# Reordering the steps of a pipelined graph network: one-hots and GpSimd operations placed anew

## The chip, the cores and the metric

The kernel runs on one core of one Trainium2 chip. The metric is the device time in microseconds, the median over several runs. One core has five engines with instruction queues of their own: PE (TensorE), DVE (VectorE), ACT (ScalarE), POOL (GpSimd) and SP (SyncE, here used for DMA only). Instructions of one engine run in the order in which the program issues them; between engines they are ordered by semaphores.

## The reference

128 graphs with 128 nodes and 64 features each. `x` is (128, 128, 64) and `adj` (128, 128, 128), symmetric in its pattern, with about 6% of the edges present and all self-loops. H is 192.

```python
mask = (adj > 0.0)
xj_proj = x @ W1a                                   # W1a, W1b: the halves of W1
diff = x[:, :, None, :] - x[:, None, :, :]
h  = relu(xj_proj[:, :, None, :] + diff @ W1b + b1)
hm = einsum('bjkh,bjk->bjh', h, mask)
x  = layernorm(x + hm @ W2 + sum(mask, -1)[..., None] * b2)    # layer 0

agg = adj @ x
out = elu(elu(agg @ V1 + c1) @ V2 + c2) @ V3 + c3              # 64 -> 128 -> 128 -> 64
x   = layernorm(x + out)                                       # layer 1
```

## The kernel before

**Tiling.** Two graphs make a pair; there are 64 pairs (`NP`). In layer 0 only the edges that exist are computed. For each pair the nodes are sorted by degree. The sorted nodes fall into nine blocks (`BLOCKS`), each with a fixed number of neighbour slots. For each block a one-hot matrix (`oh`, L707, written by VectorE in bf16 from `vp`, the running number of each neighbour, and `slotc`, the slot numbers) selects the neighbours.

**A unit** is one block of one pair: ScalarE writes the nodes' own part `aj` into a PSUM bank, repeated over the slots (L955), TensorE adds the neighbours' part by matmuls with the one-hots (L966, the parts `cf`, `rest` and `low` of a number split into three bf16 terms), and VectorE sums absolute values over the slots (L976). relu(z) is (z + |z|)/2, so a correction (`sa`, `ea`, `corr`) turns the sum of absolute values into the sum of relus. Three PSUM banks serve the units in turn, so a unit's write by ScalarE waits for the reduce of the unit three before.

**Threads.** What a pair needs is written as threads of steps:

- `prepare`: `mk` and the degrees (L576, VectorE), `degb` and `keyc` (L583, L584, GpSimd), a matmul that spreads the keys, the comparisons `cmp` (L597, VectorE), and the permutation `perm` (L605, VectorE).
- `sort_x`: sorted x, the projections to `aj` (L643, ScalarE), `sa` (L651, GpSimd), a short matmul, `ea` (L668, VectorE), `corr` (L674, GpSimd).
- `sort_mask`: the sorted mask, its prefix sums `vp` (L700, ScalarE), and the nine one-hots.
- `turn` and `project_c`: transposes, the neighbours' projections, `cf` (L756, ScalarE), `rest` (L760, VectorE), `low` (L764, GpSimd).
- `finish`: `hm` (L889), the product with W2, the way back to the old order of nodes, the normalization (`norm`: y L772 and st L777 on VectorE, `ve` L784, `rs` L787 on GpSimd, the scaling `x`), then layer 1 (`aggregate`, L917, two rounds of `elu` with `r`, `e`, `up` on ScalarE and `h` L841 on GpSimd), the last matmuls and the second normalization to `o`, which SyncE stores.

Work of about eight pairs is in flight at a time. For pairs from `LATE` on, `hm`, `ve`, `x` and `h` run on VectorE instead of GpSimd (`h` at L844, `x` at L801), and `o` is shared by ScalarE (L818) and VectorE (L804).

**The order.** A planner (`Flow`) runs while the program is built. It repeatedly takes the thread whose next step is due first, gives it an estimated time on its engine and emits its instructions. The due time of a step is `ROUND * p` plus an entry of the table `DUE`; `finish` of the last six pairs adds the offsets of `LAST`. The engine name "PORT" is a pseudo-engine of the planner's estimates: steps that name it are kept apart in its plan, but not on the chip. The plan sets nothing but the order of the instructions in each queue and which of the five `m` banks in PSUM a step takes.

```python
self.clock[e] = t + cost
...
due = [due[i] + later[0 if i < 4 else 1 if i < 8 else 2 if i < 16 else 3]
       for i in take]
flow.start(ROUND * p, due, gen)
```

Of the kernel before, what the change touches and what calls it, by code (L numbers as in the profile page):

```python
# [47 lines left out]
def gnn_kernel(ctx: ExitStack, tc: tile.TileContext, x, adj, w1, b1, w2, b2,  # L48
# [28 lines left out]
    with ExitStack() as fast:  # L77
        loads = fast.enter_context(tc.tile_pool(name="loads", bufs=8))
        prep = fast.enter_context(tc.tile_pool(name="prep", bufs=5))
        work = fast.enter_context(tc.tile_pool(name="work", bufs=5))  # L80
        ps_e = fast.enter_context(tc.tile_pool(name="ps_e", bufs=1, space=bass.MemoryType.PSUM))
        ps_m = fast.enter_context(tc.tile_pool(name="ps_m", bufs=1, space=bass.MemoryType.PSUM))
        K = sparse(tc, locals())
# [103 lines left out]
def sparse(tc, env):  # L187

    g = type("env", (), dict(env))
    nc, P, N, F, H, O, HB, H1, NP, E = (  # L190
        g.nc, g.P, g.N, g.F, g.H, g.O, g.HB, g.H1, g.NP, g.E)
# [11 lines left out]
    AHEAD = 4  # L203

    DUE = {
        "prepare": (-21.4113, -21.4103, -20.8009, -20.0167, -16.5154),
        "sort_x": (-11.5423, -11.5413, -2.7266, -2.3845, 0.0214, 1.3277, 2.8168, 12.6347),
        "sort_mask": (-10.347, -9.218, -8.7754, -8.3524, -5.8935, -5.758, -5.757, -5.756,
            -5.755, -5.754, -5.1217, -5.1207, 1.0998, 1.1008),
        "turn": (-26.2816, -24.1632),  # L210
        "project_c": (-13.6709, -12.5698, -12.2977, -12.2751, -11.3882, -10.0036, -8.4866),
        "finish": (13.0404, 22.189, 23.0263, 23.6287, 24.5439, 27.278, 28.4137, 32.117, 34.5413,
            35.4475, 35.4637, 36.1308, 36.1318, 36.1328, 37.7091, 43.35, 43.6764, 45.3519,
            45.5256, 46.0637, 48.8402, 49.096, 49.261, 51.6959, 51.9284),
        "unit": [(-1.48, -0.1838, 0.7496), (0.1062, 0.9216, 0.9226), (0.3987, 1.0968, 1.978),
            (1.1956, 1.4908, 2.221), (2.1682, 2.6234, 3.9141), (2.1874, 3.6496, 4.2699),
            (2.4467, 4.3465, 5.2271), (8.5772, 9.7062, 10.187), (5.7368, 9.4611, 10.7836)],
        "consts_late": (14.79, 24.13, 25.63, 26.63, 26.78, 26.79, 26.8, 26.81, 26.82, 27.82,
            28.82, 29.82, 30.82, 31.82, 32.82, 33.82, 34.82, 35.82, 36.82, 37.82, 38.82, 39.82,
            40.82),  # L220
    }

    LATE = NP - 2
    LAST = ((-3.5, -9.4, -4.9, -1.3), (5.5, -4.3, 0.3, 7.6), (-0.9, -2.8, 3.8, 7.6), (0.1, -0.2, -0.4, 5.1), (0.0, -1.6, 0.0, 0.2), (0.0, 0.0, 0.2, 0.0))

    def begin_thread(name, p, gen):
        due = DUE[name]
        if name == "finish":
            take = range(25)
            if p >= LATE:  # L230
                take = (0, 1, 2, 3, 4, 5, 6, 6, 7, 8, 9, 10, 11, 12, 14, 15, 16, 17, 19,
                        20, 21, 22, 22, 23, 24, 24)
            k = NP - 1 - p
            later = LAST[k] if k < len(LAST) else (0.0,) * 4
            due = [due[i] + later[0 if i < 4 else 1 if i < 8 else 2 if i < 16 else 3]
# [104 lines left out]
    def made(*names):  # L340
        return [event("const", name) for name in names]
# [425 lines left out]
    def norm(p, yps, ev, name, rest, shift):  # L767
# [31 lines left out]
        def apply(v, s):  # L799
# [3 lines left out]
            else:  # L803
                v.tensor_scalar(o[:, s, :], y[:, s, :], rs[:, s:s + 1], None, op0=OP.mult)  # L804
        if p < LATE:
            ev, = yield ("POOL", 1.1, [ev] + made("mhalf"), 0,
# [17 lines left out]
    def elu(p, zb, ev, name, k):  # L824
# [10 lines left out]
        h = work.tile([P, 2 * N], F32, name=name)  # L835
        if p < LATE:
            up = work.tile([P, 2 * N], F32, name="up", bufs=3)
# [11 lines left out]
    def overflow():  # L849


        v, B = nc.vector, 2 * NP

        over = slotc[:, :NB * B].rearrange("p (n b) -> p n b", n=NB)

        def before():
            for i, (p0, p1, sl) in enumerate(BLOCKS):
                v.memset(first[:, i:i + 1], float(p0))
        ev, = yield ("DVE", 0.5, [[0.0]], 0, before)

        def compare(blocks):
            for i in blocks:
                v.tensor_scalar(over[:, i, :], g.degs, float(BLOCKS[i][2]), None, op0=OP.is_gt)
        for k in range(0, NB, 3):
            ev, = yield ("DVE PORT", 0.5, [ev], 0, lambda: compare(range(k, k + 3)))

        def rows_over(t):
            for i in range(NB):
                nc.tensor.matmul(t[:B, i:i + 1], over[:, i, :], onesb[:, 0:1], start=True, stop=True)
        ev, t = yield ("PE", 0.6, [ev], 1, rows_over)  # L870
        ev, = yield ("DVE", 0.1, [ev], 0, lambda: v.tensor_tensor(hit[:B], t[:B, :NB], first[:B],
                                                                  op=OP.is_gt))
        flow.give(t, ev)
        ev, = yield ("DVE", 0.1, [ev], 0, lambda: v.tensor_reduce(bad[:B], hit[:B], AX.X, OP.max))
        ev, t = yield ("PE", 0.1, [ev], 1, lambda t: nc.tensor.matmul(
            t[:1, :B], bad[:B], identb[:B, :B], start=True, stop=True))
        ev, = yield ("DVE", 0.2, [ev], 0, lambda: v.tensor_reduce(
            count, t[:1, :B].rearrange("o (n s) -> o n s", s=2), AX.X, OP.max))
        ev, = yield ("DVE", 0.2, [ev], 0, lambda: v.tensor_reduce(some, t[:1, :B], AX.X, OP.max))
        flow.give(t, ev)  # L880

    def finish(p):

        d, xx = S[p], XX[p]
        hm = work.tile([P, 3, N], F32, name="hm", bufs=4)
        late = p >= LATE
        ev, = yield ("DVE PORT" if late else "POOL PORT", 0.47 if late else 1.05,
# [16 lines left out]
        if p == NP - 1:  # L904
            due = [DUE["finish"][i] + LAST[0][2] + 0.5 for i in (8, 12, 14, 16)]
            flow.start(ROUND * p, due[:1] * 4 + due[1:2] * 3 + due[2:3] + due[3:] * 2, overflow())
# [327 lines left out]
```

## Time and profile before

| what | us |
|---|---|
| median of 3 runs | 699.7 (699.24 to 699.98) |
| the profiled execution's own time | 699.37 |
| its span in the trace | 697.6 |
| first gather of pair 0 | 18.09 |
| first gather of pair 7 | 92.34 |
| first gather of pair 62 | 655.85 |
| first gather of pair 63 | 665.64 |
| end of the last unit's reduce | 676.92 |
| end of the span | 697.6 |

The span runs from the first to the last event that the profiler saw. A round is the time from a pair's first gather to that of the next pair. In a profile's row, a name such as `e<-oh,cf` says what is written and from what; the number in `x6` is the number of instructions. Mean granted clock of TensorE is 0.992.

The two engines with the most work follow each other closely: PE is busy for 97% of the span and DVE for 97%, ACT for 89% and POOL for 84%.

### The profile page before, as it was taken

Reading aid. Unit: us, or ns where it says so; the run is one execution under the profiler, and the core shown is the slowest. Engines: PE = TensorE matmul, PEld = TensorE weight load, DVE = VectorE, ACT = ScalarE, POOL = GpSimd, SP = SyncE. Lnnn points to the kernel's source line nnn. Section 1 sums busy time; section 2 is a strip of 40 time slices with the busy share of each in tenths; the row PEclk is TensorE's granted clock in tenths of the full one; section 3 lists DMA queues with packets and bytes.
Section 4 is the critical chain, followed back from the end, with each engine's and each line's share of the span. In section 5 each row is a group of like instructions: output and inputs, shape, how many; then the busy total and the mean of one; then the engine's idle time right before and its main releaser. Section 6 shows DMA issues by size and latency. Waiting matters only on the chain.

```text
span 697.6 us, 40860 instructions
## 1 busy us (share of the span) xinstructions
PE 676.6 (97%) x17245; PEld 610.3 (87%) x17246; DVE 674.2 (97%) x2267; ACT 621.2 (89%) x1731; POOL 583.4 (84%) x983
## 2 busy tenths in 40 slices
PE   7989999999999999999999999999999999999984
PEld 4878999999999999999999999999999999989972
DVE  6899999999999999999999999999999999999985
ACT  3678999999999999999999999999999999999963
POOL 5447988988988898898899889899888888899873
PEclk9999999999999999999999999999999999999996
DMA  3200111110110111111011011101101101100000
GB/s 93 56 3 3 35 26 27 35 34 19 34 34 19 33 34 26 27 34 34 19 35 33 23 31 34 32 20 34 34 19 33 34 23 30 35 22 9 12 9 20
DMA packets 54988, 20.01 MB, mean 29 GB/s; under 512 B 37904, under 2 KB 54800, under 8 KB 54800
## 3 DMA queue, kind: packets, MB, share of 16 engines
q1 hardware_dynamic: 54096, 17.06, 10.1%
q8 instruction: 137, 2.24, 1.3%
q14 instruction: 51, 0.42, 0.2%
q10 hardware_dynamic: 704, 0.30, 0.2%
HBM read 13.14 MB, written 4.19 MB: 25 GB/s over the span
## 4 chain that ended last, share of the span: by engine, by line
PE 90%; DVE 4%; POOL 2%; ACT 2%; issue 1%; DMA 1%; SPq 0%; POOLq 0%; DVEq 0%; ACTq 0%
PE e L966 46%; PE m L263 23%; PE m L741 4%; PE m L636 3%; PE m L722 3%; PE m L917 2%; PE m L619 2%; PE m L632 2%; DVE sums L976 1%; PE m L657 1%; PE m L661 1%; PE m L723 1%; POOL rs L787 1%; ACT e L955 1%; DVE oh L707 1%
## 5 line engine op out<-in xcount | busy, mean ns | idle before, releaser
L955 ACT COPY e<-aj 128x504 f32<-128x504 f32 (+6 forms) x576 | 311.3, 551 | 39.1 <-DVE sums L976 36.9
L976 DVE TENSOR_REDUCE sums<-e 128x54 f32<-128x486 f32 (+8 forms) x576 | 336.8, 603 | 3.5 <-PE e L966 2.1
L966 PE MATMUL e<-oh,cf 128*64 128x162 bf16 (+6 forms) x3456 | 210.9, 229 | 4.3 <-ACT e L955 4.0
L966 PE MATMUL e<-oh,rest 128*64 128x162 bf16 (+6 forms) x3456 | 209.0, 227 | 0.0
L966 PE MATMUL e<-oh,low 128*64 128x162 bf16 (+6 forms) x3456 | 209.0, 227 | 0.0
L966 PEld LDWEIGHTS <-cf 128*64 128x64 bf16 x3456 | 150.3, 110 | 30.7 <-issue 29.8
L707 DVE TENSOR_TENSOR oh<-vp,slotc 128x336 bf16<-128x336 bf16 (+6 forms) x576 | 155.9, 325 | 0.3 <-ACT vp L700 0.3
L966 PEld LDWEIGHTS <-rest 128*64 128x64 bf16 x3456 | 141.4, 110 | 0.0
L966 PEld LDWEIGHTS <-low 128*64 128x64 bf16 x3456 | 141.1, 110 | 0.3 <-POOL low L764 0.3
L841 POOL TENSOR_TENSOR h<-up,e 128x256 f32<-128x256 f32 x124 | 95.9, 774 | 10.4 <-ACT up L839 10.3
L787 POOL TENSOR_TENSOR rs<-ve,mhalf 128x2 f32<-128x2 f32 x128 | 92.0, 719 | 13.9 <-DVE ve L784 3.5
L764 POOL TENSOR_TENSOR low<-rest 128x512 bf16<-128x512 f32 x64 | 66.6, 1040 | 9.8 <-DVE rest L760 9.8
L651 POOL TENSOR_TENSOR sa<-aj,srow 128x384 f32<-128x384 f32 x64 | 65.6, 1025 | 8.1 <-DVE perm L605 4.0
L889 POOL TENSOR_TENSOR hm<-sums,corr 128x384 f32<-128x384 f32 x62 | 62.3, 1005 | 4.9
L674 POOL TENSOR_TENSOR corr<-ea,sa 128x384 f32<-128x384 f32 x64 | 65.3, 1020 | 0.0
L831 ACT ACTIVATE r<-m,cc 128x256 f32<-128x256 f32 x128 | 61.8, 483 | 3.5 <-PE m L263 3.3
L839 ACT ACTIVATE up<-m,cc 128x256 f32<-128x256 f32 x124 | 58.0, 468 | 0.0
L834 ACT ACTIVATE e<-r 128x256 f32<-128x256 f32 x128 | 53.4, 417 | 2.2
L760 DVE TENSOR_TENSOR rest<-m,cf 128x256 f32<-128x256 f32 x128 | 51.9, 407 | 0.0
L784 POOL TENSOR_SCALAR ve<-st 128x2 f32<-128x2 f32 x124 | 33.6, 271 | 20.5 <-DVE st L777 9.6
L756 ACT COPY cf<-m 128x256 f32<-128x256 f32 x128 | 41.4, 377 | 7.2 <-PE m L263 5.5
L643 ACT ACTIVATE aj<-m,b1n 128x128 f32<-128x128 f32 x128 | 40.0, 364 | 3.7 <-PE m L636 2.2
(163 smaller groups left out, 1459.4 us busy)
## 6 DMA issues: line engine op xcount, KB each, us to landing
adj<-in_adj_dram SPq DMA_DIRECT2D x64, 128.0 KB, 2.5
xx<-in_x_dram SPq DMA_DIRECT2D x64, 64.0 KB, 2.2
out_dram<-o SPq DMA_DIRECT2D x64, 64.0 KB, 1.7
w1s<-in_L_gnn_W_dram ACTq DMA_DIRECT2D x2, 96.0 KB, 2.9
w2s<-in_L_gnn_W_dram ACTq DMA_DIRECT2D x2, 48.0 KB, 2.5
v2s<-in_L_gnn_W_dram SPq DMA_DIRECT2D x1, 64.0 KB, 2.1
v1d<-in_L_gnn_W_dram SPq DMA_DIRECT2D x2, 32.0 KB, 2.0
rows<-in_L_gnn_b_dram SPq DMA_DIRECT2D x1, 64.0 KB, 5.5
```

The lines of the kernel that those rows point to most:

```text
L263: nc.tensor.matmul(out[h], lhsT[:, h], rhs, **kw)
L651: evs, = yield ("POOL PORT", 1.0, [have] + made("srow"), 0, lambda: nc.gpsimd.tensor_mul(sa, aj, srow))
L674: ev, = yield ("POOL PORT", 1.05, [ev, evs], 0, lambda: nc.gpsimd.tensor_sub(corr, ea, sa))
L707: lambda: nc.vector.tensor_tensor(oh[:, 2 * base:2 * (base + n)].rearrange("p (b s w) -> p b s w", b=2, w=w), vp[:, :, p0:p1].rearrange("p ...
L764: lambda: nc.gpsimd.tensor_sub(flat(low), flat(rest), upper(flat(rest))))
L787: nc.gpsimd.tensor_tensor(rs, ve, mhalf, op=OP.pow)
L831: lambda: nc.scalar.activation(r, z, AF.Relu, bias=c, scale=-1.0))
L841: ev, = yield ("POOL PORT", 0.64, [ev, evr], 0, lambda: nc.gpsimd.tensor_add(h, up, e))
L889: lambda: (nc.vector if late else nc.gpsimd).tensor_sub(hm, d["sums"], d["corr"]))
L955: lambda: nc.scalar.copy(e.rearrange("p (c s w) -> p c s w", c=3, w=w), d["aj"][:, :, p0:p1].rearrange("p c (o w) -> p c o w", o=1) .to_br ...
L966: nc.tensor.matmul(e[HALVES[h], c * n:(c + 1) * n], cp(k, s, slice(chunk * HB, (chunk + 1) * HB)), oh[:, 2 * base + s * n:2 * base + (s + ...
L976: nc.vector.tensor_reduce(d["sums"][:, :, p0:p1], e.rearrange("p (c s w) -> p c w s", c=3, w=w), AX.X, OP.add, apply_absolute_value=True)
```

## The change

The tables of due times are replaced, `LATE` becomes `NP - 3`, and the offsets `LAST` are new. No other line changes.

```diff
     DUE = {
-        "prepare": (-21.4113, -21.4103, -20.8009, -20.0167, -16.5154),
-        "sort_x": (-11.5423, -11.5413, -2.7266, -2.3845, 0.0214, 1.3277, 2.8168, 12.6347),
-        "sort_mask": (-10.347, -9.218, -8.7754, -8.3524, -5.8935, -5.758, -5.757, -5.756,
-            -5.755, -5.754, -5.1217, -5.1207, 1.0998, 1.1008),
-        "turn": (-26.2816, -24.1632),
-        "project_c": (-13.6709, -12.5698, -12.2977, -12.2751, -11.3882, -10.0036, -8.4866),
...
+        "prepare": (-28.364, -26.9206, -21.7812, -19.6952, -16.1672),
+        "sort_x": (-10.9988, -6.9662, -5.6912, -4.4256, -4.4082, -2.3787, -2.259, 9.8274),
+        "sort_mask": (-10.5624, -9.3935, -7.0848, -6.4931, -5.7683, -4.7121, -4.6732, -4.6722,
+            -4.6712, -4.6702, -4.6692, -4.6472, -4.5393, 5.8821),
+        "turn": (-28.2283, -26.8089),
+        "project_c": (-16.5622, -15.4251, -15.3192, -15.3182, -14.9622, -14.9612, -12.1988),
...
-    LATE = NP - 2
-    LAST = ((-3.5, -9.4, -4.9, -1.3), (5.5, -4.3, 0.3, 7.6), (-0.9, -2.8, 3.8, 7.6), (0.1, -0.2, -0.4, 5.1), (0.0, -1.6, 0.0, 0.2), (0.0, 0.0, 0.2, 0.0))
+    LATE = NP - 3
+    LAST = ((0.3, -1.6, -3.1, -6.4), (1.6, -5.3, 3.3, 1.7), (0.0, -0.3, 3.3, 2.9), (-0.2, -2.6, 1.3, 12.5), (0.0, 0.0, 0.0, 0.2), (0.0, -0.2, 0.2, -0.1))
```

The other rows of the table ("finish", "unit", "consts_late") change in the same way. What it makes of a round in the steady part:

| engine | order of one round before | order of one round after |
|---|---|---|
| VectorE | reduce, mk, reduce, two one-hots (308, 340), reduce, rest, reduce, y, reduce, cmp, ea, three reduces with y and st, five one-hots, perm, two one-hots, two reduces, rest | reduce, y, reduce, st, cmp, y, st, reduce, mk, reduce, one-hot (340), reduce, perm, eight one-hots, three reduces, both rest, ea, reduce |
| GpSimd | low, h, ve, rs, ve, rs, o, x, x, sa, degb, keyc, h, corr, hm | low, hm, ve, rs, ve, rs, degb, keyc, sa, o, h, x, x, corr, h |

Numbers behind a one-hot are its width per partition. On TensorE the same matmuls stand in a new order: the keys are now spread for the pair two ahead, the products with W2 belong to the pair one before (formerly two), and the last matmuls of layer 1 to the pair five before (formerly four). Before the first gather, pairs 0 to 4 have their sorting begun. SyncE's transfers keep their order. For pair 61, `hm`, `ve`, `x`, `h` and `o` move from GpSimd to VectorE and ScalarE.

More of the change, by code (lines that the diff above doesn't have):

```diff
@@ L205, in sparse @@
     DUE = {
-        "prepare": (-21.4113, -21.4103, -20.8009, -20.0167, -16.5154),
-        "sort_x": (-11.5423, -11.5413, -2.7266, -2.3845, 0.0214, 1.3277, 2.8168, 12.6347),
-        "sort_mask": (-10.347, -9.218, -8.7754, -8.3524, -5.8935, -5.758, -5.757, -5.756,
-            -5.755, -5.754, -5.1217, -5.1207, 1.0998, 1.1008),
-        "turn": (-26.2816, -24.1632),
-        "project_c": (-13.6709, -12.5698, -12.2977, -12.2751, -11.3882, -10.0036, -8.4866),
-        "finish": (13.0404, 22.189, 23.0263, 23.6287, 24.5439, 27.278, 28.4137, 32.117, 34.5413,
-            35.4475, 35.4637, 36.1308, 36.1318, 36.1328, 37.7091, 43.35, 43.6764, 45.3519,
-            45.5256, 46.0637, 48.8402, 49.096, 49.261, 51.6959, 51.9284),
@@ L215, in sparse @@
[L215 to L220, printed above, removed]
-    }
-    LATE = NP - 2
@@ new lines, in sparse @@
+        "project_c": (-16.5622, -15.4251, -15.3192, -15.3182, -14.9622, -14.9612, -12.1988),
+        "finish": (12.0143, 19.7325, 21.228, 22.6795, 25.4688, 25.7115, 26.9458, 32.0952,
+            33.6526, 33.7611, 40.9781, 42.3303, 43.3416, 43.3426, 43.3436, 46.9845, 49.8648,
+            49.8658, 49.9751, 51.7232, 54.1076, 55.6658, 56.012, 56.8405, 62.6693),
+        "unit": [(-1.48, -0.8399, 0.0964), (-2.3263, -1.8323, -0.6051), (-0.0402, 1.6109,
+            4.5299), (4.9257, 5.1183, 6.0165), (1.0308, 4.5372, 5.2005), (5.432, 5.9284,
+            6.7121), (6.5714, 7.1469, 7.2669), (5.8429, 6.8181, 6.8735), (7.9072, 8.9869,
+            10.4225)],
@@ L226, in begin_thread @@
+        "consts_late": (12.33, 29.98, 31.48, 32.48, 32.63, 32.64, 32.65, 32.66, 32.67, 33.67,
+            34.67, 35.67, 36.67, 37.67, 38.67, 39.67, 40.67, 41.67, 42.67, 43.67, 44.67, 45.67,
+            46.67),
+    }
+    LATE = NP - 3
+    LAST = ((0.3, -1.6, -3.1, -6.4), (1.6, -5.3, 3.3, 1.7), (0.0, -0.3, 3.3, 2.9), (-0.2, -2.6, 1.3, 12.5), (0.0, 0.0, 0.0, 0.2), (0.0, -0.2, 0.2, -0.1))
     def begin_thread(name, p, gen):
```

## The prediction

> **What bounds the kernel now.** I read the page first, then the spans of equal work (windows), then the waits, then single rounds in the timeline. Busy shares and the chain of the page:
>
> ```profile
> PE 676.6 (97%) x17245; PEld 610.3 (87%) x17246; DVE 674.2 (97%) x2267; ACT 621.2 (89%) x1731; POOL 583.4 (84%) x983
> PE 90%; DVE 4%; POOL 2%; ACT 2%; issue 1%; DMA 1%; SPq 0%; POOLq 0%; DVEq 0%; ACTq 0%
> ```
>
> TensorE and VectorE are both at 97%, and TensorE carries the chain. The windows (steady part, the round of pair 62, that of pair 63, the end):
>
> ```profile
> core 0: us, PE busy (x) PEld busy (x) DVE busy (x) ACT busy (x) POOL busy (x), PEclk, DMA share, GB/s
> 92.30:655.90 563.60, 563.43 (x14798) 516.27 (x14796) 561.32 (x1870) 529.92 (x1486) 500.73 (x825) 1.00 0.12 29
> 665.60:677.00 11.40, 9.43 (x254) 8.49 (x248) 9.59 (x19) 7.80 (x21) 8.36 (x15) 1.00 0.04 9
> 677.00:697.60 20.60, 9.81 (x128) 6.37 (x126) 11.13 (x49) 7.24 (x19) 7.69 (x14) 0.73 0.09 20
> ```
>
> In the steady part TensorE is always in work (563.43 of 563.60), at full clock. Counting from the first gather of each pair, 55 rounds take 563.51 us, 10.246 each. But most take 10.205, and about every fifth takes some 10.38. So 10.205 is what TensorE needs, and about 2.1 us in rounds 8 to 61 are something else. The last pair's round has 1.97 us without TensorE work. The timeline of a slow round, DVE and POOL, then TensorE:
>
> ```profile
> 329.99 0.36 DVE L976 TENSOR_REDUCE sums<-e 128x9 f32<-128x198 f32 x1
> 330.27 1.12 DVE L707 TENSOR_TENSOR oh<-vp,slotc 128x308 bf16<-128x308 bf16 x2
> 330.38 0.81 POOL L841 TENSOR_TENSOR h<-up,e 128x256 f32<-128x256 f32 x1
> 331.32 0.40 DVE L760 TENSOR_TENSOR rest<-m,cf 128x256 f32<-128x256 f32 x1
> 331.46 0.31 PE L966 MATMUL e<-oh,low 128*64 128x112 bf16 x6
> 331.78 0.27 PE L263 MATMUL m<-identb,degb 128*64 128x128 bf16 x3
> ```
>
> and of an ordinary round:
>
> ```profile
> 319.84 0.35 DVE L976 TENSOR_REDUCE sums<-e 128x9 f32<-128x198 f32 x1
> 320.12 0.56 DVE L707 TENSOR_TENSOR oh<-vp,slotc 128x308 bf16<-128x308 bf16 x2
> 320.44 0.83 POOL L841 TENSOR_TENSOR h<-up,e 128x256 f32<-128x256 f32 x1
> 320.61 0.40 DVE L760 TENSOR_TENSOR rest<-m,cf 128x256 f32<-128x256 f32 x1
> ```
>
> The two one-hots (308 and 340 wide) take 0.56 when `h` starts 0.32 after the first, and 1.12 when `h` starts at 0.11 after it, ahead of the second: the second then waits for the whole of `h`. `rest` comes 0.5 late, the PSUM bank that it gives back comes late, and the masked matmul that takes the bank starts 0.17 late on TensorE (331.61 would be on time, by the ordinary 341.86 to 342.01). The order is a race: VectorE's own work is about 10.12 a round, less than 10.205, so it catches up until its reduce has to wait for the gather, and about every fifth round `h` gets in first. I count ten such in the steady part. Two more fall into the last round:
>
> ```profile
> 667.81 1.00 POOL L674 TENSOR_TENSOR corr<-ea,sa 128x384 f32<-128x384 f32 x1
> 668.05 1.73 DVE L707 TENSOR_TENSOR oh<-vp,slotc 128x308 bf16<-128x308 bf16 x2
> 671.03 0.40 PE L966 MATMUL e<-oh,cf 128*64 128x154 bf16 x6 [0.84 <-ACT e L955]
> ```
>
> There the pair costs 1.73 instead of 0.56, and TensorE waits 0.84 (and 0.90 once more after it) for e-banks whose reduces are late.
>
> **The change, part by part.** It changes due times only, and `LATE` from 62 to 61. TensorE gets the same matmuls and one block of fp32 projections per round as before, so the 10.205 stay. SyncE's transfers keep their order (adj lands 2.5 us after issue and is used more than a round later): nothing there.
>
> *1. VectorE's one-hots.* In the new order all eight that remain (132 to 340 wide, 1.79 us) follow `perm` (0.35) in one row; the ninth stands earlier between two reduces. GpSimd then runs low, hm, ve, rs, ve, rs, degb, keyc, sa, o, h, x, x, corr, h. I placed one round by hand from the durations of before, with 0 at the end of the 112-wide gather. That unit's reduce starts at 10.78 of the round before, `perm` at 11.19, the one-hots run from 11.54 to 13.33, the last starting at 13.10. `sa` needs `aj`, which ScalarE writes after that same reduce freed its e-bank and after two more e-writes: reduce start + 0.49 + 0.03 + 0.52 + 0.36 + 0.50 + 0.37 + 0.08 = +2.35 at the earliest (by my placing 0.3 later, at 13.43, as ScalarE has other steps between). The last one-hot starts at reduce start + 0.415 + 0.35 + 1.55 = +2.31. Both hang on one event, so if VectorE runs late, both move. Trace of before: a GpSimd operation that started even 9 ns after a one-hot began never lengthened it; those at 105 ns or more ahead did. So no collision, with at least 0.04 plus 0.1 to spare. At the other end: `hm` (the last large one) ends at 9.84 to 10.05, the next VectorE operation of the kind is the ninth one-hot at 10.52, 0.46 later. The collisions go: 10 rounds by 0.17 to 0.2 = **−2.1 us**.
>
> *2. Small GpSimd operations under the row.* ve, rs, degb, keyc now lie under one-hots. The nearest row of before:
>
> ```profile
> 336.30 1.16 DVE L707 TENSOR_TENSOR oh<-vp,slotc 128x324 bf16<-128x324 bf16 x5
> 336.16 0.70 POOL L787 TENSOR_TENSOR rs<-ve,mhalf 128x2 f32<-128x2 f32 x1
> 336.93 0.33 POOL L784 TENSOR_SCALAR ve<-st 128x2 f32<-128x2 f32 x1
> ```
>
> rs takes 0.70 there, as without one-hots (0.70 at 670.92); ve gains 0.14. So about +0.3 a round on GpSimd, which does about 9.4 of 10.2: covered. [...] Before has already seven one-hots and perm in one row, and rs passes under them. [...] Ends: 0 and +0.3 us on GpSimd, nothing on the total.
>
> *3. Is VectorE the bound?* Its sum in the new order is about 10.08 a round from starts of neighbours in before (reduces 4.7, one-hots 2.05, perm 0.35, mk and cmp 0.95, ea 0.47, two rest 0.65, y and st 0.9), 0.12 under TensorE. Nothing is added in rounds under 61. TensorE's dependencies have 0.5 to 0.9 spare: e-writes 0.55 to 0.9, h 0.6, x 0.65, banks 0.5. If that cover were gone by 0.1 it would cost 0.1 a round, 5.5 us. I take 0; ends −0.3 and +5.5.
>
> *4. The start.* More pairs are prepared before the first gather: on VectorE some 2.7 to 3.8 us of cmp, perm, oh, ea ahead of the first reduce. It stood idle there for 2.86 (11.2 to 14.1) and 1.58 (18.4 to 20.0). First reduce by hand 22.5 instead of 20.0; afterwards there is that much less to do in rounds 0 to 6, where VectorE sets the pace and has four collisions (0.14 to 0.81). 22.5 + 68.8 of work to pair 7, + 1 to 2 for idle and collisions = 92.3 to 93.3, against 93.64 for that reduce now. `sa` and `low` of the first pairs can meet one-hots at other places. I take 0 ± 1.2.
>
> *5. The end.* Pair 63's round lasts 11.28 to its last reduce; without 0.61 + 0.54 of collisions and with the pipeline one round deeper (less of other pairs' work left in it) about 8 to 9. But then pairs 60 to 62 have more left to finish: one more pair takes hm, ve, x, h and o on VectorE and ScalarE: 0.55 + 0.34 + 0.6 + 0.96 + 0.25, about 2.7 us, in a window where VectorE is busy 11.13 of 20.60. From there the last pair's chain is the same: hm, project, unsort, norm, aggregate, three layers, norm, out, 20 us. hm of 63 itself gets faster (1.07, with GpSimd's h beside it). I take **−2.0 ± 1.5**; the floor is −3.2.
>
> Sum: −2.1 + 0 + 0 + 0 − 2.0 = −4.1. The profiled execution has a span of 697.6 and a time of 699.37; its new time would be 695.3. The median of the three runs is 0.33 above that execution, so **695.7**, said as 696.
>
> **The rivals.** *One-hots meet `sa` (slower).* If `sa` starts more than 0.1 us ahead of the last one-hot, that one waits for it: 1.0 less nothing, about 0.95 on VectorE, whose slack is 0.12. Deciding point: the third aj against the start of the last 308-wide one-hot, −0.1 us. Once in three rounds that is 18 times 0.95 = +16 us (712); in every round, after the slack, 56 times 0.83 = +46. For it: 0.04 is a thin margin, in before 0.09 lost every fifth round. Against it: both hang on one reduce. *A new wait on TensorE.* A deeper order with banks 0.5 apart may cost 0.1 to 0.2 a round in the steady part, +5 to +11 (703 to 709 with the gains of the end partly kept); for it, VectorE at 97%; against it, no margin of mine is under 0.5. *Gains given back.* The start 1.5 later and the end no shorter, because the extra pair's finish lies on the last chain: −2.1 + 1.5 + 1 = 700. *It does not do what it says:* another GpSimd operation (x or h) drifts onto the ninth one-hot: price as before, 0.17 in some rounds, 698.
>
> **How the numbers follow.** About 0.2%, 1.4 us, can be told from no change. The sum as worked, 693 to 698: 0.62. Given back, or the race in another place, 698 to 701: 0.13, of which nearly all is "same". New wait on TensorE, 701 to 709: 0.13. Collision with sa, 705 and up: 0.12. Faster 0.62, same 0.12, slower 0.26. The likeliest case alone is 693 to 698. To leave out no more than 2 in 10, the range runs from 693 to 705.
>
> **What would show it.** Right: all rounds from pair 7 at 10.20 to 10.21, no one-hot over its usual time by more than 0.1, `sa` starting just behind the last one-hot's start, the last round near 9, VectorE waiting for TensorE once a round. Wrong: one-hots of 308 at 1.2 us, or a TensorE wait in each round; a first gather after 21 with the seventh after 93; a stretch longer than 20.6 from the last reduce to the end.

## The result and the profile after

The kernel after takes **692.05 us** (median of 4 runs, 691.63 to 692.78), the kernel before on the same chip 699.47. The ratio is 0.9895, with a 95% interval of 0.9878 to 0.9912. The change makes it faster by about 7.4 us; 4.0 had been forecast (699.7 to 695.7), and the measured time lies 0.95 below the low end of the range. The profiled execution has a span of 689.9 us and its own time is 691.63. Line numbers of the kernel after are higher by one.

First the page (busy times and chain), then the windows over the same stretches of work as before: pair 7's first gather to pair 62's, pair 63's round, and from the last reduce to the end:

```profile
PE 667.1 (97%) x17245; PEld 605.8 (88%) x17246; DVE 667.9 (97%) x2275; ACT 621.7 (90%) x1730; POOL 553.1 (80%) x975
PE 87%; DVE 6%; ACT 3%; issue 1%; DMA 1%; POOL 1%; SPq 0%; POOLq 0%; DVEq 0%; ACTq 0%
```

```profile
92.37:650.47 558.10, 558.05 (x14799) 513.84 (x14795) 555.38 (x1868) 530.18 (x1485) 476.49 (x824) 1.00 0.12 29
660.17:669.30 9.13, 8.47 (x238) 7.86 (x232) 8.37 (x21) 7.40 (x18) 6.29 (x12) 1.00 0.08 17
669.30:689.90 20.60, 9.32 (x149) 6.31 (x143) 11.65 (x55) 8.55 (x23) 7.50 (x13) 0.80 0.09 20
```

TensorE is still always in work in the steady part (558.05 of 558.10), with as many instructions as before, yet the same 55 rounds are shorter by 5.4 us. Laid beside the trace of before:

| stretch | before | after | difference |
|---|---|---|---|
| start to first gather of pair 0 | 18.09 | 18.96 | +0.87 |
| from there to first gather of pair 7 | 74.25 | 73.41 | −0.84 |
| to first gather of pair 62 | 563.51 | 558.10 | −5.41 |
| round of pair 62 | 9.79 | 9.70 | −0.09 |
| pair 63 to its last reduce | 11.28 | 9.12 | −2.16 |
| last reduce to the end | 20.68 | 20.61 | −0.07 |
| span | 697.6 | 689.9 | −7.7 |

A pair's first gather is counted from the load of its first weights. In the new order that gather is another one (66 columns wide instead of 162), so the marks of the first and the last stretches are not at quite the same work; the 55 rounds between pair 7 and pair 62 are not touched by this.

Every one of rounds 8 to 60 takes 10.14 to 10.15 (median 10.151; round 61, with less work left, 9.97). Before, the median was 10.207, and about every fifth round took some 10.38. One steady round of the kernel after in the timeline, VectorE and GpSimd:

```profile
301.08 0.43 DVE L606 TENSOR_TENSOR perm<-iotf,pos 128x256 f32<-128x256 f32 x1
301.05 0.69 POOL L788 TENSOR_TENSOR rs<-ve,mhalf 128x2 f32<-128x2 f32 x1
301.44 1.66 DVE L708 TENSOR_TENSOR oh<-vp,slotc 128x324 bf16<-128x324 bf16 x7
303.24 0.62 DVE L977 TENSOR_REDUCE sums<-e 128x33 f32<-128x462 f32 x1
303.28 1.01 POOL L652 TENSOR_TENSOR sa<-aj,srow 128x384 f32<-128x384 f32 x1 [1.07 <-ACT aj L645]
```

This is the forecast picture: the one-hots stand in one row at their usual length (none in the steady part is over the median of its width by more than 0.02), `rs` runs across `perm` and the row's start in 0.69, and `sa` waits for ScalarE's `aj` and starts behind the start of the last one-hot (303.02). What was not forecast is on TensorE. Starts of consecutive groups, first two places of before, then the same two groups after:

```profile
316.98 0.23 PE L263 MATMUL m<-b2p,onesb 128*64 128x64 bf16 x4
317.04 0.63 PE L263 MATMUL m<-h,v2s 128*64 128x256 f32 x4
317.50 0.39 PE L619 MATMUL m<-perm,xx 128*64 128x128 f32 x4
...
319.41 0.26 PE L966 MATMUL e<-oh,low 128*64 128x66 bf16 x6
319.50 0.41 PE L917 MATMUL m<-turned,x 128*64 128x128 f32 x4
319.75 0.39 PE L966 MATMUL e<-oh,cf 128*64 128x168 bf16 x6
```

```profile
306.61 0.38 PE L967 MATMUL e<-oh,low 128*64 128x162 bf16 x6
306.82 0.39 PE L918 MATMUL m<-turned,x 128*64 128x128 f32 x4
307.04 0.39 PE L620 MATMUL m<-perm,xx 128*64 128x128 f32 x4
...
308.26 0.39 PE L967 MATMUL e<-oh,low 128*64 128x168 bf16 x6
308.48 0.60 PE L264 MATMUL m<-h,v2s 128*64 128x256 f32 x4
308.91 0.39 PE L967 MATMUL e<-oh,cf 128*64 128x168 bf16 x6
```

A group here is a run of matmuls of one product; its time is counted from its start to the start of the next group. The product h·v2s takes 0.46 before and 0.43 after, the aggregate product (turned, x) 0.25 and 0.22. Summed over the medians of all groups of a round, TensorE needs 10.207 before and 10.150 after. Two groups make up that difference, h·v2s (0.462 to 0.432) and the aggregate (0.247 to 0.217). Some gathers differ too, by 0.10 where they stand ahead of the transposes and by 0.025 where they stand behind the products with `wc`; these costs only move from one gather to another. No other group differs by more than 0.004.

Before, each of these fp32 groups stands directly behind short bf16 matmuls (64 and 66 columns); after, behind gathers of 162 and 168 columns. Within the group, the second pair of matmuls is late: in the aggregate it starts 0.137 behind the first, where 0.109 is usual, and in h·v2s 0.246, where 0.216 is usual. The rows of the weight loads (PEld), before and after:

```profile
317.01 0.20 PEld L263 LDWEIGHTS m<-h,v2s 128*64 128x64 f32 x4
319.48 0.20 PEld L917 LDWEIGHTS m<-turned,x 128*64 128x64 f32 x4
```

```profile
306.75 0.21 PEld L918 LDWEIGHTS m<-turned,x 128*64 128x64 f32 x4
308.40 0.22 PEld L264 LDWEIGHTS m<-h,v2s 128*64 128x64 f32 x4
```

The first load starts with the matmul before the group: 0.028 ahead of the group's first matmul behind a short neighbour, 0.07 behind a long one. In the slow places the load of the second pair starts 0.056 to 0.058 behind the first load, and so 0.028 to 0.030 behind the first matmul; elsewhere it starts 0.002 to 0.003 behind it.

### The profile page after: what moved, and what is told of

Read it like the earlier page. It is cut to its first block, busy times and chain, and to the rows that moved or that the text cites. A ratio compares the mean times of both kernels' runs of the same rounds, so it can differ in the third digit from the quotient of the medians.

```text
span 689.9 us, 41107 instructions
## 1 busy us (share of the span) xinstructions
PE 667.1 (97%) x17245; PEld 605.8 (88%) x17246; DVE 667.9 (97%) x2275; ACT 621.7 (90%) x1730; POOL 553.1 (80%) x975
## 4 chain that ended last, share of the span: by engine, by line
PE 87%; DVE 6%; ACT 3%; issue 1%; DMA 1%; POOL 1%; SPq 0%; POOLq 0%; DVEq 0%; ACTq 0%
PE e L967 46%; PE m L264 22%; PE m L742 4%; PE m L723 3%; PE m L637 3%; DVE sums L977 2%; PE m L620 2%; PE m L918 2%; PE m L633 2%; DVE oh L708 1%; PE m L658 1%; ACT e L956 1%; PE m L662 1%; PE m L724 1%; PE m L664 0%
## 5 line engine op out<-in xcount | busy, mean ns | idle before, releaser
L977 DVE TENSOR_REDUCE sums<-e 128x9 f32<-128x198 f32 (+8 forms) x576 | 332.4, 603 | 3.9 <-PE e L967 1.3
L956 ACT COPY e<-aj 128x504 f32<-128x504 f32 (+6 forms) x576 | 299.4, 544 | 39.7 <-DVE sums L977 38.4
L967 PE MATMUL e<-oh,cf 128*64 128x66 bf16 (+6 forms) x3456 | 210.9, 228 | 6.0 <-ACT e L956 5.8
L967 PE MATMUL e<-oh,rest 128*64 128x66 bf16 (+6 forms) x3456 | 209.0, 227 | 0.0
L967 PE MATMUL e<-oh,low 128*64 128x66 bf16 (+6 forms) x3456 | 209.0, 227 | 0.0
L967 PEld LDWEIGHTS <-cf 128*64 128x64 bf16 x3456 | 143.6, 110 | 42.6 <-issue 32.1
L708 DVE TENSOR_TENSOR oh<-vp,slotc 128x336 bf16<-128x336 bf16 (+6 forms) x576 | 143.1, 309 | 1.2 <-ACT vp L701 1.2
L842 POOL TENSOR_TENSOR h<-up,e 128x256 f32<-128x256 f32 x122 | 89.2, 731 | 3.5 <-ACT up L840 3.5
L761 DVE TENSOR_TENSOR rest<-m,cf 128x256 f32<-128x256 f32 x128 | 47.3, 408 | 0.0
L742 PE MATMUL m<-wc,turned 64*64 64x256 f32 x512 | 40.6, 381 | 0.5 <-ACT aj L645 0.4
```

Source lines behind the costliest of these rows:

```text
L708: lambda: nc.vector.tensor_tensor(oh[:, 2 * base:2 * (base + n)].rearrange("p (b s w) -> p b s w", b=2, w=w), vp[:, :, p0:p1].rearrange("p ...
L742: nc.tensor.matmul(cps[s][h, :cols], d["turned"][k, 2, h], wc[k, :], start=True, stop=False)
L842: ev, = yield ("POOL PORT", 0.64, [ev, evr], 0, lambda: nc.gpsimd.tensor_add(h, up, e))
L956: lambda: nc.scalar.copy(e.rearrange("p (c s w) -> p c s w", c=3, w=w), d["aj"][:, :, p0:p1].rearrange("p c (o w) -> p c o w", o=1) .to_br ...
L967: nc.tensor.matmul(e[HALVES[h], c * n:(c + 1) * n], cp(k, s, slice(chunk * HB, (chunk + 1) * HB)), oh[:, 2 * base + s * n:2 * base + (s + ...
L977: nc.vector.tensor_reduce(d["sums"][:, :, p0:p1], e.rearrange("p (c s w) -> p c w s", c=3, w=w), AX.X, OP.add, apply_absolute_value=True)
```

## The experiments

Theory A: the 3.2 us missing from the forecast are these two places on TensorE, 2 × 0.029 us in 55 rounds. Theory B: TensorE's order is innocent; it runs faster because other engines' work lies elsewhere.

### One place mended in the kernel before (b_one)

```diff
-        "project_c": (-13.6709, -12.5698, ...
+        "project_c": (-13.6709, -12.7298, ...
```

> The kernel before with one TensorE group moved: the bias products (b2p, 64 columns, bf16) stand between the two 154-wide gathers instead of ahead of the fp32 product h*v2s; every other queue is as it was. Theory A (an fp32 group that follows short bf16 matmuls of 64 or 66 columns loses about 0.03 us at its second weight load, at two places of a round before, at none after): ordinary rounds 10.205 -> 10.176, 63 times 0.029 = -1.8 us, and VectorE catches up more slowly, so 10 lost races become about 7 (-0.5): about 697.2. Theory B (TensorE ran faster after because the other engines' accesses fall elsewhere; its own order is nothing): unchanged, 699.5.

Measured: 696.2 us against 700.53 for the kernel before on that chip, ratio 0.9938 (0.9922 to 0.9955). All of rounds 8 to 60 are 10.18, and the product h·v2s, with b2p now ahead of the 154-wide gather, is back at 0.43:

```profile
305.18 0.23 PE L263 MATMUL m<-b2p,onesb 128*64 128x64 bf16 x4
305.24 0.37 PE L966 MATMUL e<-oh,cf 128*64 128x154 bf16 x6
...
305.85 0.59 PE L263 MATMUL m<-h,v2s 128*64 128x256 f32 x4
306.28 0.38 PE L619 MATMUL m<-perm,xx 128*64 128x128 f32 x4
```

VectorE, ScalarE and GpSimd have the order of before, instruction by instruction, so theory B cannot explain the faster product. One thing went further than expected: in the steady part no race is lost at all, where about 7 were expected. So the gain of 4.3 us is more than the product's: 55 × 0.026 = 1.4 us come from it, and 2.1 from the races. In this trace VectorE waits about 0.06 in every round at the end of its row of one-hots and keeps step with 10.18; `h` starts 0.09 to 0.10 behind the 340-wide one-hot in every round. Why these waits came about is not shown.

### Both places mended, first attempt (b_two)

```diff
-        "project_c": (-13.6709, -12.5698, ...
+        "project_c": (-13.6709, -12.7298, ...
-        "finish": (..., 32.117, 34.5413, ...
+        "finish": (..., 32.117, 34.365, ...
```

> As b_one, and the aggregate product (turned, x; fp32) is moved too, from behind the 66-wide gather to ahead of it, behind 128-wide bf16 matmuls. Theory A: ordinary rounds 10.147 as in the kernel after, -3.6 us, and VectorE, at 10.12 of its own, gains only 0.03 a round, so that about 3 or 4 races are lost instead of 10 (-1.2): about 694.7. Theory B: unchanged, 699.5.

Measured: 729.49 us, ratio 1.0407 (1.0389 to 1.0424). The expectation failed, and usefully. Moved ahead of the 66-wide gather, the aggregate product makes TensorE wait about 0.13 in each round. A steady round:

```profile
309.53 0.40 POOL L797 TENSOR_TENSOR x<-x,rs 128x128 f32<-128x128 f32 x1
309.90 0.41 DVE L760 TENSOR_TENSOR rest<-m,cf 128x256 f32<-128x256 f32 x1
310.43 0.23 PEld L917 LDWEIGHTS m<-turned,x 128*64 128x64 f32 x4
310.46 0.44 PE L917 MATMUL m<-turned,x 128*64 128x128 f32 x4
```

Its input `x` has been there for 0.5 by then. By the semaphores it waits for `rest`, which ended 0.15 earlier and gives back a PSUM bank; so it is in 48 of 50 steady rounds. With this wait the phases of the engines shift, and the 340-wide one-hot loses its race in every round. Groups by form in the steady part, before and b_two (count, busy time, mean ns):

```profile
L707 DVE TENSOR_TENSOR oh<-vp,slotc 128x340 bf16<-128x340 bf16 x53 | 22.6, 426 | 0.0
```

```profile
L707 DVE TENSOR_TENSOR oh<-vp,slotc 128x340 bf16<-128x340 bf16 x50 | 43.9, 878 | 0.0
```

878 ns instead of some 335 is 0.54 more on VectorE in each round, and the rounds are 10.74: 0.54 over 10.207. A race lost now and then cost 0.17 a time in the kernel before, since VectorE makes up the rest; lost in every round of b_two, it costs all 0.54.

### Both places mended, without a new wait (b_two2)

```diff
-        "project_c": (-13.6709, -12.5698, ...
+        "project_c": (-13.6709, -12.7298, ...
-        "sort_mask": (-10.347, ...
+        "sort_mask": (-10.185, ...
```

> The kernel before with both TensorE places mended without making any step wait for a later input: b2p between the two 154-wide gathers (as in b_one), and the masked and transposing products (perm, 128 columns, bf16) moved from ahead of the 66-wide gather to behind it, so that the aggregate product follows 128-wide matmuls. Other queues as before. Theory A: rounds 10.18 -> 10.152, -1.8 us against b_one: about 694.5 where before is 699.5, if the one-hots keep winning their race as they did in b_one; each lost race adds 0.17. Theory B (one of the two places is not what it seems, b_one's gain came from the races alone): rounds stay at 10.18, 696.

Measured: 696.35 us against 699.89, ratio 0.9951 (0.9935 to 0.9968). The rounds are 10.15 to 10.17 but for three of 10.27 or 10.28, in which `sa` meets a 308-wide one-hot. From the first gather of pair 0 to that of pair 62 it takes 0.85 less than b_one. The median round is 10.157 against 10.181, so the second place is worth about 0.025 a round, as theory A has it. The total does not show it against b_one: a first gather 1.2 us later (19.02 against 17.78) and an end 0.5 longer take it away in this profile.

### Both places put back in the kernel after (a_two), and one of them alone (a_v1p)

```diff
-            33.6526, 33.7611, 40.9781, ...
+            33.6526, 33.7611, 40.445, ...          # a_two and a_v1p
-        "unit": [(-1.48, -0.8399, 0.0964), (-2.3263, -1.8323, -0.6051), ...
+        "unit": [(-1.48, -0.8399, -0.6051), (-2.3263, -0.81, 0.0964), ...   # a_two only
```

> The kernel after with both places put back: agg*v1p (fp32) directly behind the 64-column bias products, and the aggregate product directly behind the 66-wide gather (units 162 and 66 swapped on TensorE and VectorE); nothing else moves. Theory A: rounds 10.147 -> 10.205, 62 times 0.058 = +3.6 us: about 695.6, with no one-hot lengthened. Theory B: 692.05, unchanged.

> The kernel after with one TensorE group moved and no other queue touched: agg*v1p (fp32) directly behind the 64-column bias products, ahead of the 169-wide gather. Theory A: one late weight load a round, 10.147 -> 10.177, 60 times 0.03 = +1.8 us: 693.9. Theory B: 692.05. The run a_two mixed this with a swap of two units that brought waits of its own; this one is free of them.

a_two: 710.85 us, ratio 1.0148 (1.0131 to 1.0165) to the kernel before, where 695.6 or 692 had been expected. Its rounds are 10.42. The two late weight loads are there (agg·v1p 0.467 instead of 0.435, the aggregate 0.247), but the swap of the units put further waits of about 0.2 a round on TensorE (at the keys and around v3s). So its total says little about the two places.

a_v1p is the clean one: 695.33 us, ratio 0.9932 (0.9915 to 0.9948) to the kernel before; after had 0.9895. Rounds are 10.17 to 10.19, median 10.184, against 10.151. From pair 7 to pair 62 it takes 559.97 against 558.10, +1.87. (The rest of the difference in the profiles, 1.9, lies in the start and the end.) The group that was moved, a_v1p and after:

```profile
304.71 0.23 PE L264 MATMUL m<-b2p,onesb 128*64 128x64 bf16 x4
304.77 0.63 PE L264 MATMUL m<-agg,v1p 128*64 128x128 f32 x8
305.23 0.39 PE L967 MATMUL e<-oh,cf 128*64 128x169 bf16 x6
```

```profile
303.54 0.60 PE L264 MATMUL m<-agg,v1p 128*64 128x128 f32 x8
303.97 0.39 PE L264 MATMUL m<-w2t,hm 128*64 128x128 f32 x4
```

0.46 against 0.43: the loss comes with the neighbour, in a third group that did not have it in either kernel, and no order but TensorE's has changed. Theory A stands.

### `sa` 0.37 us earlier (a_sa)

```diff
-        "sort_x": (-10.9988, -6.9662, -5.6912, -4.4256, -4.4082, ...
+        "sort_x": (-10.9988, -6.9662, -5.6912, -4.5, -4.4082, ...
```

> The kernel after with one swap on ScalarE: the three aj ahead of the copy of turned, so that sa on GpSimd starts about 0.37 us earlier, some 0.17 ahead of the last one-hot's start instead of 0.20 behind it. [...] If a margin of this kind does not matter, as under the small operations: 692, unchanged.

Measured: 717.02 us, ratio 1.0231 (1.0214 to 1.0248). In the timeline of a collided round the last four one-hots take 1.85 instead of 1.03:

```profile
239.63 1.85 DVE L708 TENSOR_TENSOR oh<-vp,slotc 128x336 bf16<-128x336 bf16 x4
240.22 1.08 POOL L652 TENSOR_TENSOR sa<-aj,srow 128x384 f32<-128x384 f32 x1 [0.90 <-ACT aj L645]
```

`sa` started 0.12 to 0.19 ahead of the last one-hot, which was longer by 0.79. That is the price of the prediction's slower rival. But it happens only in about every second round (10.22 and 10.80 alternate for long stretches), so the loss is 25 us. The author's estimate for a collision in every round was about 40, that is 732: 0.8 on VectorE (the 1.0 of `sa` less its lead), less the 0.08 that VectorE's own 10.07 leaves in a round of 10.15, is 0.72 in each of 56 rounds. The spared rounds do not differ by the lead. The same row in the round before:

```profile
229.52 1.04 DVE L708 TENSOR_TENSOR oh<-vp,slotc 128x336 bf16<-128x336 bf16 x4
230.12 1.30 POOL L652 TENSOR_TENSOR sa<-aj,srow 128x384 f32<-128x384 f32 x1 [1.06 <-ACT aj L645]
```

Here too `sa` started 0.13 ahead of the last one-hot, but it is `sa` that waits: 1.30 instead of about 1.0. Between 110 and 650 us the one-hot lost 28 times, with leads of 0.12 to 0.19, and `sa` 23 times, with leads of 0.13 to 0.19. So the start times of a trace do not tell which of the two will wait; what decides it stays open. In each of these 51 rounds one of the two paid, `sa` 0.12 to 0.19 ahead; in the kernel after `sa` starts later than that, 0.07 to 0.39 behind the last one-hot's start.

### The race alone (b_row), and in the last round alone (b_last)

```diff
-            -5.755, -5.754, -5.1217, -5.1207, 1.0998, 1.1008),
+            -5.755, -5.754, -5.1217, -5.1207, -5.1197, -5.1187),    # b_row: all pairs; b_last: pair 63
```

> The kernel before with the two one-hots that race (308, 340) moved to the end of the row behind perm: nine one-hots in one block, TensorE, ScalarE and GpSimd as before. It takes the race away and leaves TensorE's two late weight loads. If the race costs what the trace of before shows (10 times 0.17 to 0.2 in the steady part, and the two in the last round 1.7): all rounds 10.205, -2.1 in the steady part and about -1.5 at the end, 696. If the longer row now meets o and x on GpSimd, which start when the row used to end (o about 0.04 us ahead of the eighth one-hot), new stretched one-hots appear and the rounds stay at 10.2 or above: 699 or more.

> The kernel before with that move for pair 63 alone: its two last one-hots join the row of the round before, so that nothing collides in the last round. If the two collisions there (0.61 and 0.54 on VectorE, waits of 0.84 and 0.90 on TensorE) are what made the last round long: from 11.28 to about 9.6, -1.7 us: 698. If the last round is short in the kernel after because its pipeline is one round deeper: unchanged, 699.5.

b_row: 709.96 us, ratio 1.0136 (1.0115 to 1.0157). The second case of its expectation came true. Clean rounds are 10.21, but about a third of the steady ones are near 10.6, 5.1 us in all: the longer row reaches into `o` and `x`. As much again, 5.2 us, is lost before the first gather of pair 7 (79.48 against 74.25 from pair 0's), which the expectation had left out.

```profile
645.14 1.47 DVE L707 TENSOR_TENSOR oh<-vp,slotc 128x308 bf16<-128x308 bf16 x4
645.51 0.45 POOL L797 TENSOR_TENSOR o<-y,rs 128x128 f32<-128x128 f32 x1
645.92 0.48 POOL L795 TENSOR_TENSOR x<-y,st 128x128 f32<-128x128 f32 x1
```

`o` and `x` there start 0.12 and 0.14 ahead of a one-hot, which is then longer by about 0.2 each time; `rs`, a little earlier, lengthened none, but took 1.00 itself, instead of 0.70, in a third of its cases. One row of one-hots alone is not the remedy: what follows on GpSimd must move as well, as it does in the kernel after.

b_last: 699.55 us against 700.10, ratio 0.9995 (0.9977 to 1.0014): no difference that can be told. In the trace pair 63's round is 10.36 instead of 11.28. So collisions account for 0.92 of the 2.16 that the round lost; the other 1.24 is the rest of the new order, of which this run says nothing more. In this profile the end is shorter by 0.6 too, but a first gather at 19.00 instead of 18.09 and 0.5 more up to pair 7 hide both in the total. The order of the start is unchanged: the first gather varies by about 1 us between executions (17.78 to 19.02 in the five profiles that keep the old start).

### The third late pair (a_late62), and VectorE's slack (a_st)

```diff
-    LATE = NP - 3
+    LATE = NP - 2              # a_late62
-            ..., 25.4688, 25.7115, ...
+            ..., 25.4688, 26.93, ...       # a_st; and the first sa behind the next low
```

> The kernel after with LATE = NP - 2 again: pair 61 finishes on GpSimd as in the kernel before, all else as after. If the third late pair is worth something at the end: +0.3 to +1.0 us, 692.7. If the shorter end comes from the order alone (no collision in the last round, the pipeline deeper): 692.0, or less, since VectorE has 2.7 us less to do.

> The kernel after with two small moves: on VectorE the first st stands behind the next reduce instead of directly behind its y (y's step to the next start is 0.317 there and 0.198 where another operation stands between: 0.11 of VectorE per round), and on GpSimd the very first sa stands behind the next low, so that it does not hold up a one-hot for 0.8 us at 18.2. If TensorE sets the new round (my reading), rounds stay 10.147 and only the start gains, up to 1 us: about 691.3. If VectorE sets it, rounds go to 10.05 and the time to about 686.

a_late62: 692.13 us, ratio 0.9893 (0.9874 to 0.9911), against 0.9895 for the kernel after. `LATE` is worth nothing that can be told here; the work that it moves to VectorE, some 2.7 us by the prediction's estimate, does not lengthen the chain.

a_st: 693.45 us, ratio 0.991 (0.9894 to 0.9927). Its rounds are 10.151, as in the kernel after, though VectorE has 0.10 less to do in each (from `y` to the next start it takes 0.217 instead of 0.317). So TensorE sets the new round, not VectorE. The total is not better: from the last reduce to the end it takes 21.6 instead of 20.6, where `st` of the last pair now stands behind another pair's `h`, and the first gather came 1.0 later in this profile.

### The end and the start reordered (a_tail, a_best)

At its end the kernel checks that the blocks' slots suffice for the degrees found. In the chain of the kernel after, the comparisons of degrees for this check (they are written to `slotc`) hold up an `h` on VectorE, and pair 63's product with v1p is queued behind the product that needs this `h`:

```profile
675.52 1.17 DVE L864 TENSOR_SCALAR slotc<-degs 128x128 bf16<-128x128 f32 x8
676.61 0.47 DVE L845 SCALAR_TENSOR_TENSOR h<-m,cc,e 128x256 f32<-128x256 f32 x1
677.14 0.45 PE L264 MATMUL m<-v3s,h 128*64 128x64 f32 x8 [0.53 <-DVE h L845]
677.42 0.61 PE L264 MATMUL m<-agg,v1p 128*64 128x128 f32 x8
```

```diff
-            flow.start(ROUND * p, due[:1] * 4 + due[1:2] * 3 + due[2:3] + due[3:] * 2, overflow())
+            flow.start(ROUND * p, [14.5] * 3 + [27.0] + [40.74] * 3 + [43.9] + [45.0] * 2, overflow())
...                                # started at the head of finish; LAST[0][1] -1.6 -> -2.7
+     made("srow") + ([event("cp", 1)] if p == 0 else [])        # a_best: the first sa behind the next low
```

> The kernel after with the end reordered, as its chain suggests: the nine comparisons of degrees (slotc, 1.2 us on VectorE, which there hold up an h that pair 63's products with v1p queue behind) are placed in VectorE's waits for rs, ve of pair 63 ahead of another pair's h, and the bias row of the check behind pair 63's second product on TensorE. The stretch from the last reduce to the end was 20.6; 1.2 + 0.45 + 0.35 could go: about 690.2. If those operations only cover another wait (h of pair 61, which comes late anyway): 691.5 to 692.

> a_tail, and the very first sa on GpSimd behind the next low, so that the one-hot at 18.2 is not held up for 0.8 us (st stays where it is in the kernel after). If VectorE carries the start: another 0.3 to 0.8 us: about 689.7. If TensorE's first gathers wait for something else there: as a_tail, 690.2.

a_tail: 691.67 us, ratio 0.9881 (0.9866 to 0.9897). From the last reduce to the end it takes 19.5 instead of 20.6, about half of what was hoped for: `x` of pair 63 still waits for `rs`. a_best: **690.67 us**, ratio 0.9869 (0.9853 to 0.9884); pairs 0 to 7 take 72.93 instead of 73.41, and no one-hot is stretched anywhere. Its interval overlaps that of the kernel after, so the lead of 1.4 us over it rests on the medians and on these two stretches of the traces.

## Why the prediction was right or wrong

It had the direction and the mechanism of most of the gain, and half of its size. By its own steps:

- *"So 10.205 is what TensorE needs" and "TensorE gets the same matmuls ..., so the 10.205 stay"*: **this is the step that failed.** The matmuls are the same, but their order is not, and 10.205 held two late weight loads. The prediction put the change of TensorE's own round at nothing; the round fell from 10.207 to 10.151, which is worth 55 × 0.056 = 3.1 us in the steady part. b_one, b_two2 and a_v1p show it from both sides. The second place could be seen before: 0.25 between starts, against 0.22 for the product (perm, xx) of the same shape. I had summed starts to next starts for VectorE in its new order, but had carried TensorE's over as they stood, each measured behind its old neighbour.
- *1. VectorE's one-hots*, −2.1: right in the sum. 563.51 − 55 × 10.207 = 2.1 us of excess before, none after. The count was not complete: the ten collisions of `h` make up about 1.6 of it, and two of `sa` with a 308-wide one-hot, at 473.7 and 617.2, the other 0.5. The sum holds all the same, since 2.1 had been read from the rounds and not from the count. In the steady part `sa` starts 0.07 to 0.39 behind the last one-hot's start, mostly 0.25, where 0.04 to 0.33 had been worked out; a_sa shows what an earlier start would have cost.
- *2. Small GpSimd operations under the row*, 0: right for VectorE and for the total. In the kernel after `rs` takes 0.69 to 0.70 in 105 of 110 cases and `ve` 0.19, while `degb` takes 0.26 instead of 0.18 and `keyc` 0.31 instead of 0.19. That `rs` goes unhindered is not general: in b_one it took 1.00 in 41 of 108 cases. In the collided rounds one-hots were longer by 0.54 beside `h`, by 0.61 beside `corr`, by 0.79 beside `sa` in a_sa and by about 0.2 beside `o` and `x` in b_row; beside `rs`, `ve`, `degb` and `keyc` alone none was longer by more than 0.024 in the traces of before and after. In the spared rounds of a_sa the one that started first by the trace, `sa`, is the one that waits (1.30 instead of about 1.0).
- *3. Is VectorE the bound?*, 0: right. a_st takes 0.10 from VectorE and the round does not move.
- *4. The start*, 0: +0.87 − 0.84 = +0.03, inside the ± 1.2, but partly by the choice of the mark: counted by the 162-wide gather in both kernels, pair 7 comes 0.57 later, and the last round is shorter by 0.6 more. By hand the first reduce was to come 2.5 later. It came 1.3 later in this profile (21.30 against 20.00), and at 22.1 to 22.5 in the four other profiles that keep the new start (a_late62, a_v1p, a_sa, a_tail).
- *5. The end*, −2.0: −2.16 for the last round and −0.07 for what follows it. That the last chain keeps its 20 us was right, and the third late pair does neither harm nor good.

The sum of steps 1 to 5 gives −4.1, and the 3.1 of TensorE's own round makes −7.2; the trace has −7.7.

Of the rivals, the one-hots that meet `sa` did not come about, and a_sa put the price at 25 us. A new wait on TensorE did not come about in this change, but it did in b_two and a_two. No other GpSimd operation lengthened a one-hot in the steady part; in the whole kernel one is, at 18.2, by the first `sa`.

## What to carry to other kernels

TensorE was busy all but without a gap in the steady part of both kernels (563.43 of 563.60 us and 558.05 of 558.10), and the same matmuls took 10.207 a round in one order and 10.150 in the other. Where a busy engine's time per round is to be told, sum the starts to next starts group by group, look for the same shape with two different times, and ask what stands in front of the slower one. When two queues race with a margin of 0.1 us, mend the order so that both sides hang on the same event with more room than that, and check what the shifted row runs into next: the same edit in b_row moved the collision instead of removing it. In b_two a reordering that made one step wait 0.13 us lost a race in every round: 10.74 instead of 10.207.

## What was not expected of the hardware

Three fp32 products lost about 0.03 us at their second pair of weights where they stood behind bf16 matmuls of 64 or 66 columns. In the aggregate product the second pair of matmuls starts 0.137 behind the first there (before, behind 66 columns) and 0.108 behind it after, where the gather ahead has 162 columns; in h·v2s it is 0.246 behind 64 columns and 0.216 behind 168. agg·v1p takes 0.46 behind 64 columns in a_v1p, 0.439 behind 128 in before and 0.435 behind 169 in after. The waits of the profile show none of this; the starts of the loads do. In the slow groups of before the first load starts 0.028 ahead of the group's first matmul and the second load 0.056 to 0.058 behind the first load: 0.058 − 0.028 = 0.030, which is the loss. For agg·v1p behind 128 columns the first load starts 0.054 ahead, and the second 0.057 behind the first: 0.003, about what that group loses. Why the second load starts when it does is not shown, since no run changed the loads themselves; that the neighbour makes the loss is shown by b_one, b_two2 and a_v1p.

Where `h`, `sa`, `o` or `x` (128 to 384 columns) started 0.1 to 0.2 us ahead of a one-hot on VectorE in these runs, one of the two took longer. It was the one-hot for `h` (by 0.54, ten times in rounds 8 to 61 of before, with leads of 0.14 to 0.15, and in every round of b_two), for `o` and `x` in b_row (by about 0.2, with leads of 0.12 and 0.14), and for `sa` in 28 of 51 rounds of a_sa (by 0.79); in the other 23 it was `sa`, by about 0.3, at the same leads. The trace of before has both too: two `sa` in its start, 0.17 and 0.18 ahead (at 27.3 and 36.6), took 1.35 and 1.36 themselves and lengthened no one-hot, so "those at 105 ns or more ahead did" does not hold for all. Two-column operations (`rs`, `ve`, `degb`, `keyc`) crossed whole rows; the one-hots beside them alone were at most 0.024 over the median of their width. They took longer themselves at times: `rs` up to 1.00 instead of 0.70, `keyc` 0.37 instead of 0.19, and `ve` 1.40 instead of 0.19 twice, at 469.7 and 613.3 of before.
